# A conv + GRU kernel: which DMA queues carry the first x chunks, the biases and the weights

## The chip, the cores and the metric

The kernel runs on one core of a Trainium2 chip. The metric is the device time of one execution in microseconds (us), given as the median of several runs. Profiles are of one execution; in them, times count from the first instruction.

PE is TensorE (matmuls; PEld its weight loads), DVE is VectorE, ACT is ScalarE, POOL is GpSimd, SP is SyncE. SP and ScalarE issue DMAs on hardware queues, POOL on the software queue.

## The reference

For 16 sequences of 256 time steps and 512 channels, all in float32: a causal depthwise convolution over time with 16 taps, a residual, a GRU whose first state is `cond`, and a second residual. B = 16 batches, and the 16 rows of `cond_2048` are both the taps of the convolution and the first states.

```
x = x + conv(x, cond_2048[:, None, :])          # 16 taps, depthwise, causal
def cell(h, x):
    gi = x @ W_ih + b_ih
    gh = h @ W_hh + b_hh
    i_r, i_z, i_n = split(gi, 3); h_r, h_z, h_n = split(gh, 3)
    r = sigmoid(i_r + h_r); z = sigmoid(i_z + h_z)
    n = tanh(i_n + r * h_n)
    return (1 - z) * n + z * h
x = x + scan(cell, cond_2048, x)                # 256 steps in sequence
```

x is (16, 256, 512), W_ih and W_hh are (512, 1536), the biases are (1536,).

## The kernel before

**Tiles and stages.** Time is cut into 16 chunks of 16 steps (`CHUNKS`), 256 columns each. A chunk of x comes from memory in natural layout (`x_nat`, line 122) in 8 DMAs of 64 KB: two parities of the time step (s) by four blocks of 128 channels (j). DVE turns it into channel-major layout (`xT`, line 224, two halves of 0.7 us), ScalarE copies the last 15 steps of the chunk before in front of it (line 220) and makes the first term of the convolution (line 241), and DVE adds the other 15 taps for each of four channel blocks, 60 `tap` instructions a chunk (line 267), which gives `x1T`. For chunk 0 two of the four channel blocks are done on PE instead, with diagonal matrices that ScalarE makes from an identity (lines 290 and 294; the identity comes from POOL).

**Products.** `wih_n`, `wih_rz` and `whh[R]`, `whh[N]`, `whh[Z]` hold the weights in SBUF; each is loaded in four DMAs, one for each quarter of 32 partitions (line 173), of 256 KB, or 512 KB for `wih_rz`. Every product reads all four quarters of its weights. `ni_units` (line 322) make the n part of x1 @ W_ih for 8 steps at a time, `pair_units` (line 385) the r and z parts for two steps.

**A step** (`step`, from line 405) issues on PE, in this order: 32 products h @ W_hh for r, 32 for n, 32 for z (all line 420), then `other_products`: one or two units each of `pair_units` and `ni_units` for later steps. DVE: `seen(r)` (line 400), rn = r * h_n (446), a transpose (448), n (450), the transpose of z (459), h - n (465), and the scans that make the new h in `hist` (472). ScalarE: sigmoid of r (437), tanh (457), sigmoid of z (463), evictions. The next step's r product needs the new h.

**The order of the work around it** is written out by hand (manual schedule): each engine and each DMA queue runs its instructions in program order. Before step 0 come, for PE, 108 idle products, the convolution of chunk 0, the spread biases (line 364), the first `ni_units` and `pair_units`; for DVE, the turn of chunk 0, taps, the turn of chunk 1, taps. The taps and turns of later chunks go through a plan (`bulk`, class `Plan`, line 45): a list of units with a cost in us and the step by which they are due. `bulk.run(0, HEAD)` runs units up to a cost of HEAD before step 0, and `bulk_work` in each step runs some more, at the rate that the due times call for and up to `ROOM` = 2.05. `bulk_work` stands before the glance and rn of its step on DVE. A chunk's turn and first terms (`ahead`) stand among the taps of the chunk before, ahead of its last ten (`AHEAD`); only chunk 2's stand behind chunk 1's taps, due four steps later (lines 597 to 601). Chunk 2's x is loaded behind the sigmoid of z in step 1 (line 635).

**The queues before.** Of x chunk 0, parity 0 goes over SP and ScalarE in turn, parity 1 over POOL (line 144); of chunk 1, parity 0 over SP and parity 1 over POOL (line 157). Two bias rows follow on SP, the third bias on POOL (lines 158 to 164). W_ih's quarters 0 and 1 go over SP, 2 and 3 over POOL (line 184). W_hh's are issued in the program behind the convolution (lines 576 to 580): quarter 0 over SP, 1 over ScalarE, 2 and 3 over POOL, and R's quarter on ScalarE waits for the first quarter of W_ih n. At most eight DMAs of the hardware queues together, and eight of the software queue, are under way: the next one on the same semaphore waits for the one before it to land.

Of the kernel before, what the change touches and what calls it, by code (L numbers as in the profile page):

```python
# [32 lines left out]
GT = 8  # L33
R, Z, N = 0, 1, 2
CHUNKS = (16,) * 16
PAD = 108
HEAD = 11.0
SYNC = mybir.DependencyInfo(mybir.DependencyClass.Sync, mybir.DependencyReason.DATA)
Q_PE = (2, 3)
NI = 8  # L40
# [35 lines left out]
def conv_gru_kernel(  # L76
# [10 lines left out]
    nc = tc.nc  # L87
# [31 lines left out]
    def load_x(c, queues=((nc.sync,), (nc.sync,)), behind=None):  # L119

        n = CHUNKS[c]
        t = xin.tile([P, max(CHUNKS) // 2, P], F32, tag="x_nat", name=f"x_nat_{c}")
        for s in range(2):
            for j in range(NQ):
                made = queues[s][j % len(queues[s])].dma_start(  # L125
                    out=t[32 * j + B * s : 32 * j + B * s + B, 0 : n // 2],
                    in_=x[:, starts[c] + s : starts[c] + n : 2, j * P : (j + 1) * P],
                )
                if s == j == 0 and behind is not None:
                    tc.add_manual_dep(made.ins, behind.ins.name, SYNC, reason="later in time")  # L130
        x_nat[c] = t
# [8 lines left out]
    for j in range(NQ):  # L140
        (nc.sync, nc.scalar)[j % 2].dma_start(
            out=cond_nat[32 * j : 32 * j + B, :], in_=cond[:, j * P : (j + 1) * P]
        )
    load_x(0, ((nc.sync, nc.scalar), (nc.gpsimd,)))
    nc.scalar.activation(warm, warm, AF.Sigmoid)
    ident = const.tile([P, P], F32)
    make_identity(nc, ident)
# [6 lines left out]
    bn_nat = const.tile([P, P], F32)  # L154
    nc.vector.memset(bn_nat, 0.0)

    load_x(1, ((nc.sync,), (nc.gpsimd,)))
    nc.sync.dma_start(out=b_two[0:1, :], in_=b_hh.rearrange("(o c) -> o c", o=1))
    nc.sync.dma_start(
        out=b_two[1:2, 0 : 2 * C], in_=b_ih[0 : 2 * C].rearrange("(o c) -> o c", o=1)  # L160
    )
    nc.gpsimd.dma_start(
        out=bn_nat[0:P:L, :], in_=b_ih[2 * C : 3 * C].rearrange("(j c) -> j c", j=NQ)
    )

# [1 line left out]
    wih_rz = const.tile([P, NQ, 2 * C], F32)  # L167
    wih_n = const.tile([P, NQ, C], F32)
    whh = [const.tile([P, NQ, C], F32, name=f"whh_{g}") for g in range(3)]

    def load_weights(w_sb, w, g, queues):
        return [
            queues[j].dma_start(
                out=w_sb[L * j : L * j + L],
                in_=w[j * P : (j + 1) * P, g * C : g * C + w_sb.shape[2]].rearrange(
                    "(q l) c -> l q c", l=L
                ),
            )
            for j in (0, 2, 1, 3)
        ]  # L180


    for tile_of, g in ((wih_n, N), (wih_rz, R)):
        of_wih = load_weights(tile_of, w_ih, g, (nc.sync, nc.sync, nc.gpsimd, nc.gpsimd))
    zero_z = [const.tile([P, NQ * B * 2], F32, name=f"zero_z_{i}") for i in range(2)]
    for t in zero_z:
        nc.gpsimd.memset(t, 0.0)
# [26 lines left out]
    def turn_units(c):  # L214

        def halo():
            xT[c] = xtp.tile([P, NQ, HALO + CMAX], F32, tag="xT", name=f"xT_{c}")
            if c:
                m = CHUNKS[c - 1] * B
                nc.scalar.copy(xT[c][:, :, 0:HALO], xT[c - 1][:, :, m : m + HALO])  # L220

        def turn(a):
            o = HALO + a * PAIR
            nc.vector.transpose(  # L224
                xT[c][:, :, o : o + GT * B].rearrange("p q (a r) -> p a q r", r=L),
                x_nat[c][:, a : a + GP].rearrange("p a (q l) -> p a q l", q=NQ),
            )
            if 2 * (a + GP) == CHUNKS[c] and 4 < c + 3 < NCH:
                load_x(c + 3)

        return [(0.0, halo)] + [
            (0.7, lambda a=a: turn(a)) for a in range(0, CHUNKS[c] // 2, GP)
        ]

    def first_terms(c):

        x1T[c] = x1p.tile([P, NQ, CMAX], F32, tag="x1T", name=f"x1T_{c}")
        n = CHUNKS[c] * B

        def first(q):  # L240
            nc.scalar.activation(  # L241
                x1T[c][:, q, 0:n],
                xT[c][:, q, HALO : HALO + n],
                AF.Copy,
                scale=last1[:, q : q + 1],
            )

        for q in range(NQ):
            firsts.append((c, q, lambda q=q: first(q)))
# [9 lines left out]
    def tap_units(c):  # L259

        n = CHUNKS[c] * B

        def tap(k, q):
            while any(item[:2] == (c, q) for item in firsts):
                firsts.pop(0)[2]()
            to = slice(lag(k) if c == 0 else 0, n)
            nc.vector.scalar_tensor_tensor(  # L267
                out=x1T[c][:, q, to],
                in0=xT[c][:, q, k * B + to.start : k * B + n],
                scalar=condT[:, q, k : k + 1],  # L270
                in1=x1T[c][:, q, to],
                op0=ALU.mult,
                op1=ALU.add,
            )

        return [
            (0.135 + n / 960.0, lambda k=k, q=q: tap(k, q)) for k in range(K - 1) for q in range(NQ)
        ]
# [28 lines left out]
    def ni_units(t0, steps):  # L307

        n = steps * B
        c, o = chunk_of(t0)  # L310
        units = []
        hold = {}

        def prod(q, kc):
            if q == 0 and kc == 0:
                hold["ni"] = nip.tile([P, NQ, NI * B], F32, tag="ni", name=f"ni_{t0}")
                for i in range(steps):
                    ni[t0 + i] = hold["ni"][:, :, i * B : (i + 1) * B]
            if kc == 0:
                hold[q] = ps_ni.tile([P, NI * B], F32, tag="pni", name=f"pni_{t0}_{q}")  # L320
            for j in range(NQ):
                nc.tensor.matmul(  # L322
                    hold[q][32 * j : 32 * j + 32, 0:n],
                    lhsT=wih_n[:, kc, j * P + q * L : j * P + q * L + L],
                    rhs=x1T[c][:, kc, o : o + n],
                    start=(kc == 0),
                    stop=(kc == NQ - 1),
                    skip_group_check=True,
                )
            if kc == NQ - 1:  # L330
                evictions.append(lambda: evict(q))

        def evict(q):
            nc.scalar.activation(  # L334
                hold["ni"][:, q, 0:n], hold[q][:, 0:n], AF.Identity, bias=bnT[:, q, 0:1]
            )

        for q in range(NQ):
            for kc in range(NQ):
                units.append(lambda q=q, kc=kc: prod(q, kc))  # L340
        return units
# [33 lines left out]
    def seed_nh(p):  # L375
        nc.scalar.copy(nh[p % 2], b_rows[:, N])
# [160 lines left out]
    bulk = Plan()  # L537
# [21 lines left out]
    taps = [fn for i, (_, fn) in reversed(list(enumerate(tap_units(0)))) if i % NQ not in Q_PE]  # L559
# [13 lines left out]
    nc.scalar.copy(b_rows, spare)  # L573
    seed_rz(0)
    seed_nh(0)
    for g in (R, N, Z):

        made = load_weights(whh[g], w_hh, g, (nc.sync, nc.scalar, nc.gpsimd, nc.gpsimd))
        if g == R:
            tc.add_manual_dep(made[2].ins, of_wih[0].ins.name, SYNC, reason="behind W_ih in time")  # L580
    for fn in ni_units(*blocks[0]):
        while evictions:
            evictions.pop(0)()
# [5 lines left out]
    for c in range(1, NCH):  # L589
        due = starts[c] - NI  # L590
        taps = tap_units(c)

        ahead = []
        if c + 1 < NCH:
            ahead = turn_units(c + 1) + [(0.0, lambda c=c: first_terms(c + 1))]
        at = len(taps) - AHEAD
        for cost, fn in taps[:at] + (ahead if c > 1 else []) + taps[at:]:
            bulk.add(cost, due, fn)
        if c == 1:
            for cost, fn in ahead:  # L600
                bulk.add(cost, due + GT // 2, fn)
    bulk.run(0, HEAD)

    h = (lambda kc: condT[:, kc, 0:B], condT[:, :, 0:B])
# [69 lines left out]
```

## Time and profile before

| | us |
|---|---|
| median of 3 runs (lowest, highest) | 1043.94 (1042.65, 1044.66) |
| the profiled execution, as timed | 1043.13 |
| its span, first to last instruction | 1041.2 |
| PE busy, DVE busy, ACT busy, POOL busy | 1023.8, 926.6, 380.2, 11.4 |
| matmuls of line 420, r and z; n | 539.4; 269.6 |
| taps of line 267 on DVE, 930 | 377.3 |

Issue to landing before step 0, by the DMA view (medians): an x piece 4.9 us on POOL, 4.3 on SP and 4.1 on ACT, in the first 34 us; a W_hh quarter 14.2 on POOL, 15.4 on SP, 9.8 on ACT.

How to read it: a busy time is the union of an engine's instructions. A row of the timeline gives the start, the length, the engine (with a q for its sequencer, which issues DMAs), the line, the operation, what it writes and reads, and how many were merged; in brackets stands how long the engine idled before it and what ended that. A row of the windows gives the stretch, the busy time of PE, PEld, DVE, ACT and POOL with the number of instructions, the granted clock of TensorE as a share of full speed, the mean busy share of the 16 DMA engines, and the rate in GB/s.

### The profile page before, as it was taken

The page shows a single profiled execution, that of the slowest core. Times are in us where ns is not written, and L with a number is a line of the kernel's source. Part 1 is how long each engine was busy: PE and PEld are TensorE (multiplying, and loading weights), DVE is VectorE, ACT ScalarE, POOL GpSimd, SP SyncE. Part 2 cuts the span into 40 slices and gives each one's busy share as a digit, 9 for nine tenths or more (in the row PEclk, how much of TensorE's full clock was granted, in tenths as well). Part 3 has the DMA queues.
Part 4 walks back from the last instruction along what each step waited for, and adds up shares of the span by engine and source line. Part 5 has one row for each costly group of instructions (what it writes and reads, how often), then busy time and mean ns, then how long its engine had stood idle before and what let it go on. Part 6 is the DMA issues. An engine that isn't in the chain of part 4 may idle for free.

```text
span 1041.2 us, 71853 instructions
## 1 busy us (share of the span) xinstructions
PE 1023.8 (98%) x32952; PEld 929.9 (89%) x32952; DVE 926.6 (89%) x3606; ACT 380.2 (37%) x1520; POOL 11.4 (1%) x27
## 2 busy tenths in 40 slices
PE   7899999999999999999999999999999999999997
PEld 7789999999999999999999999999999999999986
DVE  7899999999999999999999999999999999996555
ACT  6243433434333343433334333343333334333332
POOL 4000000000000000000000000000000000000000
PEclk9999999999999999999999999999999999999999
DMA  9320100101010010100100010010000000000000
GB/s 232 93 60 8 32 14 20 30 15 27 13 34 15 15 34 6 34 14 15 35 15 25 15 33 16 14 33 7 14 15 14 14 13 5 15 15 14 14 11 17
DMA packets 40978, 27.72 MB, mean 27 GB/s; under 512 B 6686, under 2 KB 38498, under 8 KB 40676
## 3 DMA queue, kind: packets, MB, share of 16 engines
q1 hardware_dynamic: 38612, 18.52, 7.9%
q8 instruction: 257, 4.21, 1.8%
q0 software_dynamic: 1216, 3.67, 1.3%
q10 hardware_dynamic: 848, 0.95, 0.4%
q14 instruction: 45, 0.37, 0.1%
HBM read 14.73 MB, written 8.39 MB: 22 GB/s over the span
## 4 chain that ended last, share of the span: by engine, by line
PE 96%; DVE 1%; DMA 1%; ACT 0%; issue 0%; POOL 0%; SPq 0%; DVEq 0%; POOLq 0%
PE prz L420 42%; PE pnh L420 21%; PE prz L385 20%; PE pni L322 10%; PE conv L294 1%; DMA whh<-in_L_cond_W_hh_dram 1%; DMA x_nat<-in_x_dram 0%; DVE rnT L448 0%; DVE rn L446 0%; DVE zp L459 0%; DVE n L450 0%; DVE xT L224 0%; ACT zero_z L463 0%; POOL x_nat L125 0%; DVE hist L472 0%
## 5 line engine op out<-in xcount | busy, mean ns | idle before, releaser
L420 PE MATMUL prz<-whh,hist 128*32 128x128 f32 x16320 | 539.4, 273 | 2.2 <-DVE hist L472 1.3
L420 PEld LDWEIGHTS prz<-whh,hist 128*32 128x32 f32 x16320 | 449.7, 104 | 7.3 <-DVE hist L472 5.3
L267 DVE SCALAR_TENSOR_TENSOR x1T<-xT,condT,x1T 128x256 f32<-128x256 f32 (+2 forms) x930 | 377.3, 462 | 0.6 <-ACT x1T L241 0.6
L420 PE MATMUL pnh<-whh,hist 128*32 128x128 f32 x8160 | 269.6, 273 | 0.0
L385 PE MATMUL prz<-wih_rz,x1T 128*32 128x256 f32 x4096 | 268.0, 379 | 0.0
L420 PEld LDWEIGHTS pnh<-whh,hist 128*32 128x32 f32 x8160 | 226.5, 104 | 0.0
L457 ACT ACTIVATE dn<-n 128x64 f32<-128x64 f32 x256 | 67.9, 265 | 325.1 <-DVE n L450 325.1
L385 PEld LDWEIGHTS prz<-wih_rz,x1T 128*32 128x32 f32 x4096 | 128.4, 110 | 43.8
L322 PEld LDWEIGHTS pni<-x1T,wih_n 128*32 128x32 f32 x4096 | 122.4, 110 | 43.7 <-ACT ni L334 0.8
L437 ACT ACTIVATE r<-prz 128x128 f32<-128x128 f32 x256 | 70.9, 277 | 240.5 <-PE prz L420 237.7
L322 PE MATMUL pni<-x1T,wih_n 128*32 128x128 f32 x4096 | 157.9, 273 | 0.6 <-ACT ni L334 0.6
L472 DVE TENSOR_TENSOR_SCAN hist<-zero_z,dn 128x32 f32<-128x32 f32 (+1 forms) x768 | 128.5, 216 | 0.0
L446 DVE TENSOR_TENSOR rn<-r,pnh 128x128 f32<-128x128 f32 x256 | 72.3, 282 | 38.7 <-PE pnh L420 37.4
L463 ACT ACTIVATE zero_z<-zp 128x32 f32<-128x32 f32 x512 | 90.8, 226 | 6.9
L448 DVE STREAM_TRANSPOSE rnT<-rn 128x128 f32<-128x128 f32 x256 | 79.7, 311 | 8.8
L459 DVE STREAM_TRANSPOSE zp<-prz 128x128 f32<-128x128 f32 x256 | 80.8, 316 | 0.1
L334 ACT ACTIVATE ni<-pni,bnT 128x128 f32<-128x128 f32 x128 | 46.9, 367 | 75.7 <-PE pni L322 75.7
L465 DVE TENSOR_TENSOR dn<-hist,dn 128x64 f32<-128x64 f32 x255 | 58.3, 229 | 11.4
L450 DVE TENSOR_TENSOR n<-rnT,ni 128x64 f32<-128x64 f32 x256 | 57.6, 225 | 8.9
L400 DVE COPY glance<-r 1x1 f32<-1x1 f32 x256 | 34.1, 133 | 28.3 <-ACT r L437 28.2
L373 ACT COPY prz<-b_rows 128x256 f32<-128x256 f32 x128 | 48.6, 379 | 0.0
L400 DVE COPY glance<-zero_z 1x1 f32<-1x1 f32 x256 | 36.4, 142 | 7.9
(51 smaller groups left out, 214.6 us busy)
## 6 DMA issues: line engine op xcount, KB each, us to landing
out_dram<-o SPq DMA_DIRECT2D x248, 32.0 KB, 1.7
x_nat<-in_x_dram SPq DMA_DIRECT2D x118, 64.0 KB, 3.0
whh<-in_L_cond_W_hh_dram POOLq DMA_DIRECT2D x6, 256.0 KB, 14.2
wih_rz<-in_L_cond_W_ih_dram POOLq DMA_DIRECT2D x2, 512.0 KB, 10.9
wih_rz<-in_L_cond_W_ih_dram SPq DMA_DIRECT2D x2, 512.0 KB, 12.7
whh<-in_L_cond_W_hh_dram SPq DMA_DIRECT2D x3, 256.0 KB, 15.4
whh<-in_L_cond_W_hh_dram ACTq DMA_DIRECT2D x3, 256.0 KB, 9.8
x_nat<-in_x_dram POOLq DMA_DIRECT2D x8, 64.0 KB, 4.9
```

Of the source, the lines that this page charges most:

```text
L267: nc.vector.scalar_tensor_tensor(out=x1T[c][:, q, to], in0=xT[c][:, q, k * B + to.start : k * B + n], scalar=condT[:, q, k : k + 1], in1=x ...
L322: nc.tensor.matmul(hold[q][32 * j : 32 * j + 32, 0:n], lhsT=wih_n[:, kc, j * P + q * L : j * P + q * L + L], rhs=x1T[c][:, kc, o : o + n], ...
L385: nc.tensor.matmul(rz[p % 2][32 * j : 32 * j + 32], lhsT=x1T[c][:, kc, o : o + PAIR], rhs=w_rz[:, :, j * P : (j + 1) * P], start=False, st ...
L400: nc.vector.tensor_copy(glances[i][0:1], of_scalar[0:1, 0:1])
L420: product = nc.tensor.matmul(dst[32 * j : 32 * j + m], lhsT=h[0](kc), rhs=whh[g][:, kc, j * P : (j + 1) * P], start=False, stop=(kc == NQ ...
L437: of_r = nc.scalar.activation(r, pr, AF.Sigmoid)
L446: nc.vector.tensor_mul(rn, r, pnh)
L448: nc.vector.transpose(rnT, by_part(rn))
L457: nc.scalar.activation(dn_v[:, :, :, 1], n, AF.Tanh)
L459: nc.vector.transpose(zp, by_part(pz))
L463: nc.scalar.activation(z_v[:, qs, :, 1], zp[:, qs, half], AF.Sigmoid) for qs in halves
L472: nc.vector.tensor_tensor_scan(hist_g[:, lo + at : lo + end], z[:, to], dn[:, to], 0.0, op0=ALU.mult, op1=ALU.add,)
```

## The change

The first two chunks of x go over POOL's software queue, all 16 pieces. The three bias loads go over SP, ahead of the weights. All weights are now loaded in one loop before the rest of the program, in the order W_ih n, W_ih rz, W_hh R, N, Z: quarter 0 over SP, 2 and 3 over POOL, and quarter 1 over SP, except for W_hh N and Z, where it goes over POOL. ScalarE's queue carries no weights, and the wait of R's quarter for W_ih is gone. On POOL the identity now comes behind the eight pieces of chunk 0, and the two memsets of `zero_z` behind all weight issues. HEAD is 10 instead of 11, and chunk 2's turn and first terms stand among chunk 1's taps as in the other chunks.

In the program as built, 25 instead of 27 of chunk 1's taps stand before step 0 on DVE; steps 1 to 4 have five of them each instead of five, five, four and four, counting from the bulk work of step 1; step 5 has both halves of chunk 2's turn and one tap; steps 6, 7 and 8 have five, four and three taps. Before, the halves of that turn stood in steps 7 and 8.

```diff
-HEAD = 11.0
+HEAD = 10.0
...
-    load_x(0, ((nc.sync, nc.scalar), (nc.gpsimd,)))
+    load_x(0, ((nc.gpsimd,), (nc.gpsimd,)))
...
-    load_x(1, ((nc.sync,), (nc.gpsimd,)))
+    load_x(1, ((nc.gpsimd,), (nc.gpsimd,)))
     nc.sync.dma_start(out=b_two[0:1, :], in_=b_hh.rearrange("(o c) -> o c", o=1))
...
-    nc.gpsimd.dma_start(
+    nc.sync.dma_start(
         out=bn_nat[0:P:L, :], in_=b_ih[2 * C : 3 * C].rearrange("(j c) -> j c", j=NQ)
     )
...
     def load_weights(w_sb, w, g, queues):
-        return [
+        for j in (0, 2, 1, 3):
             queues[j].dma_start(
...
-    for tile_of, g in ((wih_n, N), (wih_rz, R)):
-        of_wih = load_weights(tile_of, w_ih, g, (nc.sync, nc.sync, nc.gpsimd, nc.gpsimd))
+    for tile_of, w, g in (
+        (wih_n, w_ih, N),
+        (wih_rz, w_ih, R),
+        (whh[R], w_hh, R),
+        (whh[N], w_hh, N),
+        (whh[Z], w_hh, Z),
+    ):
+        second = nc.gpsimd if tile_of is whh[N] or tile_of is whh[Z] else nc.sync
+        load_weights(tile_of, w, g, (nc.sync, second, nc.gpsimd, nc.gpsimd))
...
-    for g in (R, N, Z):
-
-        made = load_weights(whh[g], w_hh, g, (nc.sync, nc.scalar, nc.gpsimd, nc.gpsimd))
-        if g == R:
-            tc.add_manual_dep(made[2].ins, of_wih[0].ins.name, SYNC, reason="behind W_ih in time")
...
-        for cost, fn in taps[:at] + (ahead if c > 1 else []) + taps[at:]:
+        for cost, fn in taps[:at] + ahead + taps[at:]:
             bulk.add(cost, due, fn)
-        if c == 1:
-            for cost, fn in ahead:
-                bulk.add(cost, due + GT // 2, fn)
```

## The prediction

> **What bounds the kernel now.** I read the page's list of busy slices first (PE 9 tenths or more in all slices but the first four and the last, so 256 steps of 3.92 us are bound by PE and only the start is open), then the chain of waits over the first 40 us, then the timeline of each engine there, then the windows with the DMA share. The chain (start, us, what) says what sets the first step:
>
> ```profile
> 9.09 11.82 PE conv L294 x64
> ...
> 22.33 9.64 DMA whh<-in_L_cond_W_hh_dram
> 31.97 0.25 issue
> 32.22 2.00 PE prz L420 x29
> ```
>
> The reader is to see that the chain leaves PE, runs through one DMA, and comes back to PE: step 0 starts at 32.22, a quarter us after a piece of W_hh landed. The timeline says which piece: ScalarE's, issued at 22.33 behind its diagonals, evictions and bias copies; PE's rows, then DVE's, around it:
>
> ```profile
> 22.33 0.32 ACTq L173 DMA_DIRECT2D whh<-in_L_cond_W_hh_dram  x1
> ...
> 25.91 1.91 PE L385 MATMUL prz<-wih_rz,x1T 128*32 128x256 f32 x32
> 32.22 2.00 PE L420 MATMUL prz<-whh,condT 128*16 128x128 f32 x29 [4.40 <-DMA whh<-in_L_cond_W_hh_dram]
> ...
> 37.60 1.11 PE L420 MATMUL prz<-whh,hist 128*32 128x128 f32 x32
> ```
>
> ```profile
> 7.64 1.30 DVE L224 STREAM_TRANSPOSE xT<-x_nat 128x512 f32<-128x512 f32 x2 [3.33 <-DMA x_nat<-in_x_dram]
> ...
> 15.66 15.98 DVE L267 SCALAR_TENSOR_TENSOR x1T<-xT,condT,x1T 128x128 f32<-128x128 f32 x48
> 34.84 0.14 DVE L400 COPY glance<-r 1x1 f32<-1x1 f32 x1 [3.20 <-ACT r L437]
> 35.72 0.29 DVE L446 TENSOR_TENSOR rn<-r,pnh 128x128 f32<-128x128 f32 x1 [0.73 <-PE pnh L420]
> ```
>
> PE is done with its preparation at 27.82 and idles 4.40; DVE is done with its taps at 31.64 and idles 3.20. DVE is therefore only 3.2 us behind being the bound itself. The windows (us, busy of five engines, granted clock, DMA share, GB/s) show the transfers:
>
> ```profile
> 20.00:27.00 7.00, 6.44 (x167) 5.08 (x170) 7.00 (x19) 2.78 (x8) 0.00 (x0) 1.00 1.04 298
> 27.00:28.50 1.50, 0.82 (x16) 0.25 (x8) 1.50 (x5) 0.00 (x0) 0.00 (x0) 1.00 1.00 306
> 28.50:30.00 1.50, 0.00 (x0) 0.00 (x0) 1.50 (x5) 0.00 (x0) 0.00 (x0) 1.00 1.09 229
> 30.00:31.50 1.50, 0.00 (x0) 0.00 (x0) 1.50 (x5) 0.00 (x0) 0.00 (x0) 1.00 0.80 149
> 31.50:33.00 1.50, 0.78 (x13) 0.60 (x17) 0.15 (x1) 0.00 (x0) 0.00 (x0) 0.54 0.13 42
> ```
>
> The rate is near 300 GB/s while two queues have data and falls to 229 and 149 when ScalarE's queue is nearly alone; and the granted clock is 0.54 just when step 0 starts, so its R product takes 2.00 us where later steps take 0.87. Last, one later stall, at step 8:
>
> ```profile
> 66.66 0.51 ACT L241 ACTIVATE x1T<-xT,last 128x256 f32<-128x256 f32 x1 [0.90 <-DVE xT L224]
> 67.07 0.26 ACT L437 ACTIVATE r<-prz 128x128 f32<-128x128 f32 x1
> ```
>
> A forced half of chunk 2's transpose holds ScalarE's first term, which holds r, which holds PE's z product; from rn to rn this step takes 4.45 us (63.21 to 67.66).
>
> **The change, part by part.** Times are of the profiled execution, where step 1's first product starts at 37.60.
>
> *Weights leave ScalarE's queue.* Three issues (0.32 and 0.93 us, from 22.33) go. The first n eviction on ScalarE, at 23.72 behind them, then waits for PE alone, and PE's 0.56 wait for it at 24.14 goes: PE's preparation ends near 27.3 instead of 27.82. W_hh R's quarter becomes SP's ninth transfer, in flight by about 7 us; R must land by 28, and R's two pieces on the software queue, which stand ahead of all of N and Z, landed at 22.82 and 24.40 before. I cost R at nothing; its cover is some 3 us. So the old wait is gone, and the next in line are three: PE, DVE, and the last piece of W_hh Z.
>
> *PE.* Preparation ends about 27.3 plus what the convolution starts later (below, about 1.6, of which part runs while the matmuls are at half pace anyway): 28.5. A step is 3.92: step 1 could start at 32.4.
>
> *x over the software queue: DVE.* POOL's x pieces start at 1.30 and go out every 0.53 us, eight instead of four, so the last issue starts at 5.08 instead of 2.98. The four of before took 2.8, 3.5, 4.1 and 4.4 us to land, those from 4 to 6 us 5.5 to 5.9. Until SP's first weights (its queue now begins with the biases, whose memsets end at 2.9; weights from about 3.4) nothing competes, later they do. Bounds: 5.08+2.8 = 7.9 to 5.08+5.9 = 11.0; I take 3.9 to land, between the first and the fourth of the rows, 9.0. DVE started when the last landed at 7.37; it is 1.6 later. The identity on POOL, pushed behind the eight issues to about 6.2, delays the 16 diagonals (each 0.3 apart), but the convolution needs the first only and follows at its own pace, so it starts with xT, near 10.7: nothing. x's second chunk is through by about 15 and is wanted by DVE at 14.25+1.6: nothing, with one us of cover. DVE's 48 taps lose two of 0.40 each (12.8 us for 32): end 31.64+1.6-0.8 = 32.4. The glance and rn follow (0.07), and from rn to step 1 are 1.88 us (35.72 to 37.60): step 1 at 34.4. With the bounds 33.3 to 36.4.
>
> *The last weights.* Both chunks and W are 7.34 MB; the software queue now carries 4.72 of it, SP 2.62, with all of Z but a quarter at the software queue's end. Estimate from the windows: 0.28 MB by 4.5 us (one 64 KB piece in 0.53 us); 215 GB/s to 12 us (before 182 and 208, with half of x in 512-byte packets that took 0.05 us each against 0.25 for 4096 bytes on the software queue, by the trace's packet records); 268 to 15; 305 to about 28, where SP runs out; the remaining 0.7 MB alone at 200 (between 229 and 149): 31.5, landed by 32.4. Bounds: everything at 306 from 3 us on, 28.0; and every software landing as far from the next as before, with eight more x pieces at 0.53 and two more weight pieces at 1.5 each, 31.77+4.2+3.0 = 39.0. After the landing come 0.25 to the first product, 0.87 for z, and 1.30 (0.86+0.44 in step 1) of products behind it on PE: step 1 at 32.4+2.42 = 34.8.
>
> The latest of 32.4, 34.4 and 34.8 decides: 2.8 us earlier than 37.60. The half-rate clock, which made R take 2.00 instead of 0.87 us, costs between nothing and that 1.1; I take nothing, since the 0.56 and 0.6 us gaps of the row from 20 to 27 left the clock at 1.00 and R and N now run ahead of the wait for Z, so that PE's gap shrinks from 4.40 to about 2 us.
>
> *The plan.* 25 of chunk 1's taps run ahead instead of 27, and chunk 2's transposes move from steps 7 and 8 to step 5, where their data (issued behind step 1's z, landed eight us later at 49.30) is there four us before. Steps 1 to 4 then have five taps each; in steps 10 to 12 five taps gave rn distances of 4.01, 3.93, 3.93 and 3.81 after. From rn of step 0 to rn of step 9 it was 35.84; by these rows, with 4.08 and 3.98 of steps 1 and 2 as they are and steps 16 and 17 (3.96, 3.88: an output and three taps) for steps 8 and 9, it becomes 4.08+3.98+3.93+3.93+3.81+3.92+3.92+3.96+3.88 = 35.41: 0.4 won, mostly step 8. If the cover failed, each five-tap step would cost 0.1.
>
> *The sum*: 2.8+0.4 = 3.2 us off. The profiled execution took 1043.13 (span 1041.2 and 1.9 around it, unchanged): 1039.9. The median of the runs is 0.81 above it, so 1040.7.
>
> **Two rules against the rows.** The row: 306 GB/s with three queues at work, 149 to 229 with one. The Trainium skill, "DMA: Bandwidth & Descriptors", section "Issuing engines are not separate DMA queues", says that transfers run on the same 16 engines whoever starts them, and that another issuer saves issue time only. By it the last byte would come no earlier than now, about 33.0, and the gain would be 2.2+0.4 instead of 3.2; the row of the lone queue differs from it and I keep the row.
> The row: clock 0.54 after the idle stretch, R in 2.00 us. The skill's "TensorE: Matmul & The Clock Gate", section "Part 1: The HAM clock gate (the "warmup" mystery)", says that an idle window of about 3.4 us halves the clock. The trace agrees for the 4.40 us gap; by the rule a gap of two us costs nothing, and one that holds a whole window the 1.1 of R.
>
> **The rivals.** *x too late*: the software queue shares the engines with SP's weights, x0 lands at 11.0, and DVE takes the place of the wait. For: latencies of 5.5 in the same microseconds; DVE has only 3.2 us of idle time. Against: SP's and ScalarE's x pieces, which filled the engines from 3 us, are gone. Step 1 at 36.4, 1.2+0.4 won: 1042.3.
> *The bytes end when they ended*: the early stretch is used worse, Z lands at 34.0, step 1 at 36.4: 1042.3 too. For: the first three us carry one queue only. This is also the case in which the change hardly does what it says.
> *Slower: the software queue becomes the bound.* One mechanism: twice the x pieces and twelve weight pieces through one queue, each piece landing as far behind the other as before; Z lands at 39.0, PE waits, step 1 at 41.4: 3.8-0.4 = 3.4 lost, 1047.3. It eats the gain when Z lands at 35.6 and costs over 0.2% from 37.7. For: the software queue's pieces landed 1.2 to 3.5 apart. Against: SP's half of the engines comes free near 28.
>
> **How the numbers follow.** Forecast 0.61, x too late 0.16, bytes at the same end 0.10, slower 0.13. A measurement tells about 0.2%, 2.1 us, from no change. The forecast counts as faster, both middle rivals as the same: 0.61, 0.26, 0.13. The best bounds (DVE 33.3, no Z wait) give 4.3+0.4 off, 1039.2, and 0.5 for the spread of the runs, 1038.7; above, the middle rivals and the nearer part of the slower one: 1044.6.
>
> **What would show it.** No whh issue on ScalarE; step 0's first product before 29.5 at clock 1.0; x0 landed and DVE's first transpose near 9.0; the last wait before step 1's first product is PE on a whh DMA (Z) or on rn by DVE, and that product starts near 34.8; rn distance of step 8 near 3.96. Wrong if x0's transpose starts after 11.5, if Z lands after 35, or if step 5's transposes wait for x.

## The result, and the profile after

The changed kernel is slower: median 1050.48 us (1049.97 to 1051.6, 4 runs) against 1043.88 (1042.65 to 1044.66, 4 runs) for the kernel before on the same chip, a ratio of 1.0062 with a 95% interval of 1.0048 to 1.0076. The forecast was 1040.7, in 1038.7 to 1044.6. The profiled execution took 1050.13 us (span 1048.3), 7.0 more than before. Lines below the bias loads stand five further down: the products of a step are line 425 (420 before), `pair_units` 390 (385), the taps 272 (267), rn 451 (446).

The chain of waits of the kernel after, over the first 60 us (start, us, what):

```profile
7.70 10.53 DMA x_nat<-in_x_dram
18.22 0.28 issue
18.51 14.01 DMA wih_rz<-in_L_cond_W_ih_dram
32.52 0.28 issue
32.80 8.64 DMA whh<-in_L_cond_W_hh_dram
41.44 0.25 issue
41.69 1.91 PE prz L425 x32
43.59 1.45 PE prz L390 x16
45.05 0.44 PE pni L327 x16
45.48 0.87 PE prz L425 x32
```

There is no PE and no DVE in it from 7.70 to 41.69: it consists of three transfers of the software queue in a row. They are linked by the eight transfers that may be under way at once: a piece of x chunk 1, issued at 7.70, lands after 10.53 us, and only then does POOL issue a quarter of `wih_rz`; that lands 14 us later and lets the last quarter of W_hh Z go. In the chain, step 1's first product starts at 45.48 instead of 37.84 in the kernel before; in PE's timeline, whose rows start a little earlier because matmuls overlap, at 45.30 instead of 37.60. That is 7.7 us later, and the whole span is 7.1 us longer.

PE's timeline of the kernel after, around step 0, shows what it waits for:

```profile
32.61 1.93 PE L390 MATMUL prz<-wih_rz,x1T 128*32 128x256 f32 x32 [2.76 <-issue]
...
38.72 1.91 PE L425 MATMUL pnh<-whh,condT 128*16 128x128 f32 x32 [1.87 <-DMA whh<-in_L_cond_W_hh_dram]
41.69 1.91 PE L425 MATMUL prz<-whh,condT 128*16 128x128 f32 x32 [1.06 <-DMA whh<-in_L_cond_W_hh_dram]
...
45.30 0.95 PE L425 MATMUL prz<-whh,hist 128*32 128x128 f32 x28
```

W_hh N and Z each arrive too late, and both products take 1.91 us instead of the 0.87 of later steps. The windows of the same kernel over these two products show the granted clock (third from the end) at half:

```profile
38.50:41.50 3.00, 1.91 (x32) 1.17 (x32) 0.82 (x5) 0.00 (x0) 0.00 (x0) 0.50 0.54 119
41.50:43.50 2.00, 1.81 (x36) 1.68 (x40) 0.09 (x1) 0.26 (x1) 0.00 (x0) 0.50 0.00 0
```

DVE's timeline of the kernel after:

```profile
12.26 1.30 DVE L229 STREAM_TRANSPOSE xT<-x_nat 128x512 f32<-128x512 f32 x2 [7.83 <-DMA x_nat<-in_x_dram]
...
21.91 1.30 DVE L229 STREAM_TRANSPOSE xT<-x_nat 128x512 f32<-128x512 f32 x2 [2.96 <-DMA x_nat<-in_x_dram]
...
23.33 15.19 DVE L272 SCALAR_TENSOR_TENSOR x1T<-xT,condT,x1T 128x128 f32<-128x128 f32 x46
38.45 0.13 DVE L405 COPY glance<-r 1x1 f32<-1x1 f32 x1
40.69 0.29 DVE L451 TENSOR_TENSOR rn<-r,pnh 128x128 f32<-128x128 f32 x1 [2.11 <-PE pnh L425]
```

x chunk 0 is there at 12.14 (before 7.37), chunk 1 at 21.79 (before 11.11), and the taps end at 38.5 (before 31.64). So x costs twice: even with all weights in place, DVE would have let step 1 start only near 38.5 + 0.1 + 1.9 = 40.5. The windows of the kernel after (columns as before; the last two are the share of the 16 DMA engines and GB/s):

```profile
7.50:12.00 4.50, 0.00 (x0) 0.00 (x0) 0.00 (x0) 4.50 (x16) 2.30 (x5) 1.00 1.06 174
12.00:15.00 3.00, 1.29 (x3) 1.14 (x4) 2.67 (x6) 3.00 (x12) 1.09 (x2) 1.00 1.04 180
15.00:20.00 5.00, 5.00 (x31) 4.78 (x30) 3.95 (x13) 1.55 (x4) 1.72 (x4) 1.00 1.04 170
20.00:27.00 7.00, 6.26 (x74) 5.49 (x77) 5.09 (x21) 3.39 (x9) 3.23 (x6) 1.00 1.06 246
27.00:40.00 13.00, 7.50 (x198) 5.63 (x192) 11.59 (x31) 2.02 (x6) 1.46 (x4) 0.92 1.03 207
```

The same stretches of the kernel before, but for the one from 20 to 27 us (298 GB/s, shown in the prediction):

```profile
7.50:12.00 4.50, 2.91 (x8) 2.55 (x9) 4.29 (x11) 4.50 (x16) 3.00 (x8) 1.00 1.08 208
12.00:15.00 3.00, 3.00 (x15) 2.99 (x13) 3.00 (x10) 2.75 (x8) 1.54 (x4) 1.00 1.01 268
15.00:20.00 5.00, 5.00 (x39) 4.92 (x38) 5.00 (x21) 1.97 (x5) 0.50 (x1) 1.00 1.04 313
27.00:40.00 13.00, 8.60 (x232) 7.67 (x228) 8.87 (x29) 1.62 (x7) 0.00 (x0) 0.87 0.36 87
```

In the last of them all was nearly done. After the change the DMA engines count as fully busy throughout, yet from 7.5 to 20 us they move 170 to 180 GB/s where they moved 208 to 313, and about 200 for the 13 us in which the software queue works alone (by the packet records SP's weights are through at about 26 us). Two things need an explanation: why x is late, and why the busy engines move so little.

### The profile page after: what moved, and what is told of

Read it like the earlier page. It is cut to its first block, busy times and chain, and to the rows that moved or that the text cites. A ratio compares the mean times of both kernels' runs of the same rounds, so it can differ in the third digit from the quotient of the medians.

```text
span 1048.3 us, 71854 instructions
## 1 busy us (share of the span) xinstructions
PE 1024.2 (98%) x32952; PEld 928.4 (89%) x32952; DVE 926.5 (88%) x3606; ACT 380.7 (36%) x1520; POOL 16.1 (2%) x36
## 3 DMA queue, kind: packets, MB, share of 16 engines
q0 software_dynamic: 1600, 4.72, 2.2%
## 4 chain that ended last, share of the span: by engine, by line
PE 94%; DMA 3%; DVE 1%; POOL 1%; issue 0%; ACT 0%; DVEq 0%; POOLq 0%
PE prz L425 42%; PE pnh L425 21%; PE prz L390 20%; PE pni L327 10%; DMA wih_rz<-in_L_cond_W_ih_dram 1%; DMA x_nat<-in_x_dram 1%; DMA whh<-in_L_cond_W_hh_dram 1%; POOL x_nat L125 1%; DVE rnT L453 0%; DVE zp L464 0%; DVE rn L451 0%; ACT zero_z L468 0%; DVE n L455 0%; DVE hist L477 0%; DVE glance L405 0%
```

## The experiments

The runs came in four groups, each beside the kernel before on the same chip. A ratio is to that kernel before; x0 and x1 stand for the landing of the last piece of x chunk 0 and of chunk 1, in us.

### Which part of the change costs the time

Theories: A, x on the software queue next to SP's weights; B, the new split of the weights, with Z at the software queue's end. A1 is a form of A in which x pieces are slow because each reads rows that lie far apart in memory.

**x_only**: the kernel before, with only the 16 x pieces moved.

```diff
-    load_x(0, ((nc.sync, nc.scalar), (nc.gpsimd,)))
+    load_x(0, ((nc.gpsimd,), (nc.gpsimd,)))
...
-    load_x(1, ((nc.sync,), (nc.gpsimd,)))
+    load_x(1, ((nc.gpsimd,), (nc.gpsimd,)))
```

> The kernel before with one edit: all 16 x pieces over the software queue. Theory A (in the same microseconds, x on the software queue and weights on SP's: x is in flight longer, and everything with it): x chunk 0 lands at 11 to 12.5 instead of 7.4, the rate stays under 200 GB/s until about 20 us, and the time is 1047 to 1051, most of the loss. Theory B (only the uneven split of the weights counts, the software queue alone from 26 us): x lands near 9 and the time stays within 2 us of 1043.9.

Measured: 1052.17 us, ratio 1.0076 (1.0061 to 1.0091). x0 landed at 14.78, x1 at 25.02. DVE and PE in its timelines:

```profile
14.90 1.30 DVE L224 STREAM_TRANSPOSE xT<-x_nat 128x512 f32<-128x512 f32 x2 [10.79 <-DMA x_nat<-in_x_dram]
...
26.56 15.59 DVE L267 SCALAR_TENSOR_TENSOR x1T<-xT,condT,x1T 128x128 f32<-128x128 f32 x47
```

```profile
39.96 2.01 PE L420 MATMUL prz<-whh,condT 128*16 128x128 f32 x32 [5.54 <-DMA whh<-in_L_cond_W_hh_dram]
```

Both landings and the time are beyond what theory A expected. The move of x alone makes the whole loss: the ratio's interval overlaps that of the full change.

**x_as_before**: the reverse, the kernel after with those two lines put back.

> The changed kernel with x back on the three queues of before; biases, weights and plan as changed. Theory A: x chunk 0 lands at 7 to 8.5, the rate reaches 300 GB/s by 13 us, Z lands at 32 to 35, and the time is 1039 to 1043, faster than before. Theory B: the software queue still has 4.2 of its 4.7 MB, so only 0.5 MB at 200 GB/s, 2.6 us, is won: about 1047.9.

Measured: 1045.18 us, ratio 1.0013 (1.0003 to 1.0022). With x back on three queues about a fifth of the loss is left (1.3 of 6.2 thousandths), so B as the main cause is out; but there is no gain either, and the time lies between the two expectations. Its DMA view for 9 to 14 us shows why:

```profile
q0 software_dynamic: 275, 0.93, 102.7%
q1 hardware_dynamic: 19, 0.01, 1.5%
```

Columns are packets, MB and the share of 16 engines. Now SP's weights, queued behind x and the biases, are the ones that stand still: q1, SP's queue, moves 0.01 MB in 5 us while the software queue takes everything. PE then waits 3.86 us for `wih_rz` and 2.59 for W_hh R, and step 0 starts at 35.33 instead of 32.22, as its timeline says:

```profile
29.50 3.24 PE L390 MATMUL prz<-wih_rz,x1T 128*32 128x256 f32 x32 [3.86 <-DMA wih_rz<-in_L_cond_W_ih_dram]
35.33 1.26 PE L425 MATMUL prz<-whh,condT 128*16 128x128 f32 x29 [2.59 <-DMA whh<-in_L_cond_W_hh_dram]
```

**plan_only**: the kernel before with HEAD 10 and chunk 2's turn among chunk 1's taps, nothing else.

```diff
-HEAD = 11.0
+HEAD = 10.0
...
-        for cost, fn in taps[:at] + (ahead if c > 1 else []) + taps[at:]:
+        for cost, fn in taps[:at] + ahead + taps[at:]:
```

> The kernel before with HEAD 10 and chunk 2's turn among chunk 1's taps; queues as before. All theories: step 0 starts at 32.2 as before, the stall of step 8 goes (rn distance 3.96 instead of 4.45), 0.4 us won: 1043.1 to 1043.9.

Measured: 1044.24 us, ratio 1.000 (0.9991 to 1.0009). The plan does no harm: steps 2 to 9 take 0.4 us less from rn to rn, as forecast, which is below what the times can tell. Its queues are those of the kernel before, so its profile also shows how far two executions differ with nothing changed there: x0 landed at 8.08 and x1 at 12.19 (before 7.37 and 11.11), ScalarE's quarter of W_hh N at 34.42 (32.57), the rates from 7.5 us on were 178, 232 and 285 GB/s (208, 268, 313), and step 1 started at 39.59 (37.60). One profile for each kernel therefore does not tell landings apart that differ by less than about 2 us.

**close_rows**: the kernel after, x chunks 0 and 1 read from one batch's neighbouring rows.

```diff
-                    in_=x[:, starts[c] + s : starts[c] + n : 2, j * P : (j + 1) * P],
+                    in_=(
+                        x[2 * c + s, 0 : B * n // 2, j * P : (j + 1) * P].rearrange(
+                            "(b i) c -> b i c", b=B
+                        )
+                        if c < 2
+                        else x[:, starts[c] + s : starts[c] + n : 2, j * P : (j + 1) * P]
+                    ),
```

> The changed kernel, but the pieces of x chunks 0 and 1 are read from rows of one batch that lie 2 KB apart, 128 rows of 512 bytes for a piece, instead of 16 batches 512 KB apart: the same bytes, pieces, queues and 512-byte runs; chunks 0 and 1 so hold other values than the reference's. If the far rows make x slow (A1): the rate goes to 270 to 300 GB/s from about 5 us, x chunk 0 lands at 8 to 9.5, and the time falls to 1040 to 1045. If it is the queue's share beside SP's weights (A2): x lands at 11 to 12.5 again and the time is 1049 to 1051.

Measured: 1051.89 us, ratio 1.0074 (1.0058 to 1.0091), x0 at 14.08 and x1 at 23.94. Neighbouring rows are no faster: A1 falls.

### Halves of the partitions, or the queue

Theories: H, what is written into one half of the partitions (0 to 63 or 64 to 127) is held to about 200 GB/s, and SP's quarters (0, 1) and the software queue's (2, 3) fill different halves; Q, x pieces beside SP's weights are slow wherever they are written.

**even**: the kernel before with W_hh issued early, quarters 0 and 1 over SP and 2 and 3 over POOL; x, biases and plan as before. It is the base of two further runs.

```diff
-        of_wih = load_weights(tile_of, w_ih, g, (nc.sync, nc.sync, nc.gpsimd, nc.gpsimd))
+        load_weights(tile_of, w_ih, g, (nc.sync, nc.sync, nc.gpsimd, nc.gpsimd))
+    for g in (R, N, Z):
+        load_weights(whh[g], w_hh, g, (nc.sync, nc.sync, nc.gpsimd, nc.gpsimd))
...
-    for g in (R, N, Z):
-
-        made = load_weights(whh[g], w_hh, g, (nc.sync, nc.scalar, nc.gpsimd, nc.gpsimd))
-        if g == R:
-            tc.add_manual_dep(made[2].ins, of_wih[0].ins.name, SYNC, reason="behind W_ih in time")
```

> The kernel before, with one edit: quarter 1 of W_hh goes over SP instead of ScalarE and is issued with the other weights, so SP carries quarters 0 and 1 (partitions 0 to 63) and POOL 2 and 3 (64 to 127); x, biases and plan as before. Theory H (each half of the partitions takes about 200 GB/s, and 300 come only when two queues write to different halves): 280 to 310 GB/s from 12.5 us to the end, the last weights land at 31 to 33, DVE is the next bound, time 1039 to 1043. Theory Q (pieces of x behind weights on the software queue are slow whatever partitions they go to): the same here.

Measured: 1044.96 us, ratio 1.0001 (0.999 to 1.0011): no gain, where both theories expected 1039 to 1043. The software queue's Z landed at 33.34 and SP's last weights only at 35.68.

**same_half**: even with SP carrying quarters 0 and 2 of every weight, POOL 1 and 3. Each queue carries as many bytes as in even, but as long as the two queues stay in step both write the same half at the same time. The lines shown are against even.

```diff
-        load_weights(tile_of, w_ih, g, (nc.sync, nc.sync, nc.gpsimd, nc.gpsimd))
+        load_weights(tile_of, w_ih, g, (nc.sync, nc.gpsimd, nc.sync, nc.gpsimd))
...
-        load_weights(whh[g], w_hh, g, (nc.sync, nc.sync, nc.gpsimd, nc.gpsimd))
+        load_weights(whh[g], w_hh, g, (nc.sync, nc.gpsimd, nc.sync, nc.gpsimd))
```

> As even, but SP carries quarters 0 and 2 and POOL 1 and 3, in that order, so that both queues write to partitions 0 to 63 and then both to 64 to 127, as long as they stay in step; the same bytes, sizes and queues' loads. Theory H: near 200 GB/s where they are in step (up to 300 where they drift apart), the last weights land 3 to 8 us later than in even, and the time is 3 to 8 us longer. Theory Q: nothing changes, within 1 us of even.

Measured: 1048.62 us, ratio 1.003 (1.0019 to 1.0041). The windows of even:

```profile
15.00:20.00 5.00, 5.00 (x37) 4.92 (x37) 5.00 (x22) 1.98 (x5) 0.91 (x3) 1.00 1.04 274
20.00:27.00 7.00, 7.00 (x174) 5.92 (x176) 7.00 (x18) 2.83 (x8) 0.00 (x0) 1.00 1.03 285
```

and of same_half:

```profile
15.00:20.00 5.00, 5.00 (x39) 4.92 (x38) 5.00 (x21) 1.97 (x5) 0.90 (x3) 1.00 1.05 211
20.00:27.00 7.00, 5.87 (x150) 4.95 (x149) 7.00 (x19) 2.83 (x8) 0.00 (x0) 1.00 1.04 224
```

Same queues, same bytes, same busy engines (1.03 to 1.05): 274 and 285 GB/s where the halves differ, 211 and 224 where they meet. The last weights come at 40.18 instead of 35.68, and the intervals of the two times do not overlap. H holds for weights.

**x_upper** and **x_lower**: the kernel after with all pieces of x chunks 0 and 1 written to partitions 64 to 127, or to 0 to 63 where SP's weights go; the other half is filled with zeros.

```diff
-                    out=t[32 * j + B * s : 32 * j + B * s + B, 0 : n // 2],
+                    out=(
+                        t[
+                            64 + 32 * (j % 2) + B * s : 64 + 32 * (j % 2) + B * s + B,
+                            (j // 2) * (n // 2) : (j // 2 + 1) * (n // 2),
+                        ]
+                        if c < 2
+                        else t[32 * j + B * s : 32 * j + B * s + B, 0 : n // 2]
+                    ),
...
+    for c in (0, 1):
+        nc.vector.memset(x_nat[c][0:64, 0:GT], 0.0)
```

The lines shown are those of x_upper; x_lower has 0 in place of 64 and clears 64 to 128.

> The changed kernel, but the 16 pieces of x chunks 0 and 1 all land in partitions 64 to 127 (two columns' blocks beside each other) and partitions 0 to 63 are set to zero: the same pieces, queues and bytes from memory; the first two chunks hold other values. SP's weights of the same time go to partitions 0 to 63. Theory H: the pieces do not meet SP's weights: all of chunk 0 lands by 8.5 to 9.5 us, chunk 1 by 14 to 16, the rate from 7.5 to 15 is 230 or more, and the last weights land 4 or more us earlier than in the changed kernel (41.4). Theory Q: chunk 0 lands at 11 to 12.5, the last weights at 40 to 43.

> As x_upper, but all pieces land in partitions 0 to 63, with SP's weights, and 64 to 127 are set to zero. Theory H: chunk 0 lands after 13, chunk 1 after 22, the rate stays at or under 200 until SP is through, and the last weights land at 42 or later. Theory Q: the same landings as x_upper within 1 us.

Measured: 1051.5 us, ratio 1.0057 (1.0035 to 1.008), x0 at 13.89, x1 at 23.47; and 1054.6 us, ratio 1.0087 (1.0067 to 1.0107), x0 at 14.55, x1 at 25.85. Away from SP's half, x is as late as ever, later even than Q expected: H does not explain x, Q stands. In the half that meets SP's, x0 is 0.7 and x1 2.4 us later and the last weights land at 45.20 instead of 42.64. That is little more than the spread of two executions, so whether the half also matters for x is left open.

### What holds an x piece

Theories: S0, the pieces are slow on their own; S, each piece has its price beside SP's weights; B (here), its bytes have. L, against H: one queue alone can move only 200 GB/s, wherever it writes.

**hold**: the kernel after, SP's first weight made to wait until the last piece of x chunk 1 has landed.

```diff
-    load_x(1, ((nc.gpsimd,), (nc.gpsimd,)))
+    last_x = load_x(1, ((nc.gpsimd,), (nc.gpsimd,)))
...
-            queues[j].dma_start(
+            made = queues[j].dma_start(
...
+            if w_sb is wih_n and j == 0:
+                tc.add_manual_dep(made.ins, last_x.ins.name, SYNC, reason="behind x in time")
```

> The changed kernel with one wait more: SP's first weight waits until the last piece of x chunk 1 has landed; queues, sizes and bytes as changed. Theory Q (pieces of x on the software queue are slow because SP's weights are under way in the same microseconds): every x piece lands 2.8 to 4 us behind its issue, chunk 0 by 8 to 9 us, chunk 1 by 12 to 14, although SP's weights start 9 us later; the last weights land at 34 to 37 instead of 41.4, and the time is 1042 to 1046. Rival S0 (the software queue by itself lands a piece only every 1.4 us): chunk 0 lands at 11 or later again, the last weights at 42 or later, and the time is 1050 or more.

Measured: 1049.46 us, ratio 1.0038 (1.0025 to 1.0051). x0 landed at 8.81 and x1 at 13.45. The DMA view gives the median time to landing of single issues; first the kernel after, for the x pieces issued before 4 us, from 4 to 6 and from 6 to 9, each in its own answer:

```profile
x_nat<-in_x_dram POOLq DMA_DIRECT2D x5, 64.0 KB, 3.0
...
x_nat<-in_x_dram POOLq DMA_DIRECT2D x4, 64.0 KB, 6.1
...
x_nat<-in_x_dram POOLq DMA_DIRECT2D x5, 64.0 KB, 9.8
```

then hold, for the pieces issued from 4 to 10 us and SP's weights issued from 13 to 20:

```profile
x_nat<-in_x_dram POOLq DMA_DIRECT2D x12, 64.0 KB, 3.6
...
wih_n<-in_L_cond_W_ih_dram SPq DMA_DIRECT2D x2, 256.0 KB, 12.6
```

With SP silent each of the 16 pieces lands 2.8 to 3.7 us behind its issue, with up to seven under way at once; with SP's weights in flight those issued from 4 us on take 6 to 11. S0 falls, and Q is shown for the landings. Its last weights (34 to 37) and its time (1042 to 1046) did not come. The chain of hold says why:

```profile
9.81 3.64 DMA x_nat<-in_x_dram
...
16.02 23.57 DMA whh<-in_L_cond_W_hh_dram
```

In turn SP's weights, which come second here, wait for the software queue: the trace's packet records have no packet of SP's weights until 20 us, 6.5 us after the first issue. That ate much of what the early x had won; the last weights came at 39.6. So x in time is not enough: with x0 and x1 where the prediction had them, or earlier, the kernel is still slower than the kernel before.

**pieces8**: the kernel after, chunks 0 and 1 in 8 pieces of 128 KB instead of 16 of 64.

```diff
-    load_x(0, ((nc.gpsimd,), (nc.gpsimd,)))
+    both = const.tile([P, max(CHUNKS), P], F32, name="x_nat_01")
+    for s in range(2):
+        for j in range(NQ):
+            nc.gpsimd.dma_start(
+                out=both[32 * j + B * s : 32 * j + B * s + B],
+                in_=x[:, s : CHUNKS[0] + CHUNKS[1] : 2, j * P : (j + 1) * P],
+            )
```

> The changed kernel, but x chunks 0 and 1 come in 8 pieces of 128 KB (16 steps of one parity) instead of 16 of 64 KB, all on the software queue as there; chunk 0 is whole only with the eighth. Theory S (beside SP's weights a piece costs about 1.4 us whatever its size): the eighth lands at 14 to 17 instead of chunk 1's 21.8, and the last weights 4 or more us earlier than 41.4. Theory B (the queue gets a share of bytes or packets): the eighth lands at 20 to 23, the last weights at 40 to 43.

Measured: 1050.13 us, ratio 1.0052 (1.004 to 1.0065); the eighth piece landed at 17.90, between the two expectations, and the last weights at 37.96, 3.5 us earlier than in the kernel after and also between them. The run does not decide between S and B.

**wide**: the kernel after, each weight DMA writing one slot of all 128 partitions. The rows of W then lie in other partitions, so the products are not those of the reference.

```diff
-                out=w_sb[L * j : L * j + L],
-                in_=w[j * P : (j + 1) * P, g * C : g * C + w_sb.shape[2]].rearrange(
-                    "(q l) c -> l q c", l=L
-                ),
+                out=w_sb[:, j],
+                in_=w[j * P : (j + 1) * P, g * C : g * C + w_sb.shape[2]],
```

> The changed kernel, but each weight DMA writes 128 partitions (128 rows of W, 2 or 4 KB each) instead of 32 partitions with four rows each: the same bytes, packets, queues and order; the rows lie in other partitions, so products use permuted rows of W. Theory H (a queue alone is held at 200 GB/s by the half of the partitions that it writes to): the software queue alone, behind SP's end, moves 270 or more, and the last weights land at 35 to 38. Theory L (a lone queue moves 200 whatever it writes to): 195 to 215 GB/s in the tail, the last weights at 40 to 43. x beside SP's weights stays slow in both, unless the ports that SP's weights fill are what slows it: then chunk 0 lands before 11.

Measured: 1045.23 us, ratio 1.0001 (0.9989 to 1.0013). Its window, to be set beside 246 and 207 GB/s of the kernel after (in the packet records the software queue has 2.72 of the 2.75 MB of this stretch, so it works alone):

```profile
20.00:27.00 7.00, 7.00 (x140) 6.35 (x142) 7.00 (x27) 3.81 (x10) 2.58 (x7) 1.00 1.03 394
```

The last weights landed at 30.32 instead of 41.44, so a lone queue is not held to 200 GB/s; how many partitions its transfers write makes the difference. L falls. x remained late (10.90 and 19.25). By the expectation, x0 before 11 would mean that the ports filled by SP's weights slow it; 10.90 meets that by 0.1 us and is only 1.2 us earlier than in the kernel after, less than the spread of two executions, so this stays open. DVE became the bound, as the PE timeline of wide says:

```profile
37.76 1.94 PE L423 MATMUL prz<-whh,hist 128*32 128x128 f32 x32 [3.48 <-DVE hist L475]
```

That is step 1, 0.2 us from where the profile of the kernel before has it.

### A version meant to beat both

**even_wide**: x over three queues and W_hh early, as in even, with each weight DMA writing one slot of all partitions, and the rows taken in the order that the products need.

```diff
-                out=w_sb[L * j : L * j + L],
-                in_=w[j * P : (j + 1) * P, g * C : g * C + w_sb.shape[2]].rearrange(
-                    "(q l) c -> l q c", l=L
-                ),
+                out=w_sb[:, j],
+                in_=w[:, g * C : g * C + w_sb.shape[2]].rearrange(
+                    "(j q l) c -> q j l c", q=NQ, l=L
+                )[j],
```

> The kernel of even (the kernel before, W_hh issued early with quarter 1 over SP; x, biases and plan as before), with each weight DMA bringing the rows for one slot q of all 128 partitions instead of all slots of 32 partitions, in the layout that the program reads, so that it computes the reference. What the runs so far point to: x stays ahead of the weights in each queue, and no queue is held to the half of the partitions that it writes. Theory H: the rate after 15 us is over 300 GB/s and stays there to the end, the last weights land by 31 instead of 35.7; DVE (idle 3.20 us before the glance of step 0 in the kernel before) then becomes the bound, step 0's rn near 32.7-33.5 instead of 35.72, step 1 near 34.6-35.4 instead of 37.60: 1040.8-1042. Rival: weights that write all partitions meet x's writes in every port, x1 lands at 13-15 instead of 11.1 and DVE's taps end 2 us later; rn near 35 and 1043-1044, no gain that can be told.

Measured: 1075.71 us, ratio 1.0292 (1.0275 to 1.0308). Neither expectation came near. Its windows and SP's timeline:

```profile
20.00:27.00 7.00, 2.94 (x46) 1.92 (x48) 7.00 (x19) 1.43 (x4) 1.03 (x3) 0.73 1.11 115
34.00:46.00 12.00, 1.10 (x12) 0.22 (x12) 0.00 (x0) 0.00 (x0) 0.00 (x0) 0.50 0.26 101
```

```profile
10.36 43.13 SPq L173 DMA_DIRECT2D whh<-in_L_cond_W_hh_dram  x6
```

From 34 us on only a quarter of the DMA engines' time is used (0.26) at 101 GB/s, and SP needs 43 us to issue six transfers. Besides the queues of x and of some weights, the difference to wide is the source of a weight transfer: four groups of 32 rows with gaps, where wide has 128 rows in one run. The Trainium skill, "DMA: Bandwidth & Descriptors", section "Why a DMA increments its semaphore by 16 and not by 1", says that the number of engines that share a transfer is the largest number up to 16 that divides the outermost dimension of both sides; here these are 4 and 128, so 4 engines. The share of 0.26, some four of 16 engines, fits that; which engines were used is not in the records, and no run changed this alone. Whether H can be turned into a gain with rows in this order is left open.

## Why the prediction was wrong, point by point

| step of the prediction | forecast | measured |
|---|---|---|
| x0 landed | 9.0 (7.9 to 11.0) | 12.14 |
| x1 through | about 15 | 21.79 |
| rate to 12 us; to 15; to about 28 | 215; 268; 305 GB/s | 172-174; 180; 170, then 246 |
| rate of the lone queue | 200 GB/s | 207 |
| left for the lone queue | 0.7 MB, from 28 | 2.9 MB, from 26 |
| W_hh R landed | before 28 | 35.11 |
| DVE's taps end | 32.4 | 38.5 |
| W_hh Z landed | 32.4 (28.0 to 39.0) | 41.44 |
| Z landed to step 1 (chain) | 2.42 us | 4.04 |
| plan | 0.4 won | 0.38 won, steps 2 to 9 |

**The step that failed is the sizing of a landing without what is in flight beside it.** It stands in two terms of the sum.

*x*: "I take 3.9 to land, between the first and the fourth of the rows". Those rows were of pieces with x on the other queues beside them. Once SP has no x, its weights are in flight from about 5 us: by the packet records 0.74 MB of them from 5 to 11 us, where the kernel before has 0.26 MB, all behind 7.9 us. The x pieces issued from 4 us on then need 6 to 11 us (hold against after). The bound of 11.0 used the 5.9 of the slowest row, which had only those 0.26 MB beside it.

*The last weights*: "305 to about 28, where SP runs out; the remaining 0.7 MB alone at 200". SP ran out at about 26, but by then the software queue had moved only 1.8 of its 4.72 MB, and the other 2.9 MB took it 15 us alone. This term set the time: by DVE's path step 1 could have started near 40.5. The term of 34.8 also adds up pieces of the chain, where step 1 of the kernel before starts at 37.84, and subtracts from the timeline's 37.60; that is 0.2 us.

x_only shows that the move of x makes the loss, by both terms together. x in time alone does not turn the sign: in hold x0 landed at 8.81, within the forecast, and the time was still 1.0038 of the kernel before.

**The rates were taken as a matter of how many queues have work** ("near 300 GB/s while two queues have data"). same_half and wide show otherwise: two queues reach 211 to 224 GB/s when they write the same half, one queue 394 when it writes all partitions. The number for the lone queue, 200, was right, for the wrong reason: it is the rate of transfers that write one half. Theory H is what the Trainium skill says in "SBUF — State Buffer", section "Door 1: The DMA port swizzle": the bandwidth follows from how many of 16 ports the partitions reach, and 0 to 63 reach only half of them. The rows 285, 224 and 394 agree with it.

**The rule weighed there**, that a second issuer adds no bandwidth, holds against the row that was kept: a lone queue moved 394 GB/s in wide, and moving W_hh's quarter off ScalarE won no time in even (1.0001). The gain of 2.2+0.4 that it still allowed did not come either, since the queues do matter in another way, which neither the rule nor the prediction had: whose data was in flight first moved most of the bytes. From 5 to 15 us of the kernel after the packet records show 1.37 MB of SP's weights and 0.38 MB of the software queue. In x_as_before (9 to 14 us: 0.93 MB of the software queue, 0.01 of SP's) and in hold (13.5 to 20 us: 1.31 and none) it was the other way round.

**"I cost R at nothing; its cover is some 3 us."** R's last quarter came 7 us after 28: the software queue's R stood behind x and W_ih, so the landing of before (24.40), with eight x pieces ahead of it instead of 16, did not carry over.

**The half-rate clock "costs between nothing and that 1.1; I take nothing".** With N and Z each a gap, the clock was 0.50 for N and for Z: 1.04 us for Z and 0.59 for the products behind it, which is 1.6 of the 4.04 against 2.42. By the rule weighed there a gap of two us would have cost nothing; here PE's idle stretch before N was 1.87 us and that before Z 1.06, and the clock was 0.50 all the same from 38.5 to 43.5 us. The measurement decides against that reading of the rule.

**The rivals.** "x too late" named the mechanism, sharing with SP's weights, but stopped at 11.0. "The software queue becomes the bound" named the place, Z at 39.0 and step 1 at 41.4: the place was right, the price too low by 2.4 us of landing and the 1.6 of the clock. Both happened at once, and the prediction treated them as alternatives.

**The sum of what was measured**: step 1 is 7.70 us later by the timelines, rn of step 1 7.50 later, rn of step 9 7.12 later after the plan's 0.38, and the span 7.1 longer.

**Open**: why a piece of 64 KB waits so long beside another queue's backlog. pieces8 did not tell a price for each piece from one for bytes. Nor do the runs say how a queue keeps another out: in hold the records from 13.5 to 20 us show 48 to 50 packets of 4 KB a us for the software queue and none for SP, though SP had issued its first weights at 13.46.

## What to carry to other kernels

A transfer's time to landing holds only for what was in flight beside it; when a change takes small urgent pieces off a queue, ask first what that queue will now start earlier. For weights, look at which partitions each transfer writes before counting queues: transfers that run at the same time should write different halves, or all 128 partitions in one run of rows. And bounds of two rivals that share a cause have to be added, not chosen between.

## What was not expected of the hardware

DMA engines that count as fully busy moved anything from 115 GB/s (even_wide, 20 to 27 us) to 394 (wide, the same stretch): the share says that packets are in the engines, not that bytes move. A queue with a backlog can hold another one at next to nothing: 0.01 MB in 5 us in x_as_before. And even_wide, whose weight transfers read 4 x 32 rows where wide's read 128 in one run, took 30 us longer than wide (1075.71 against 1045.23); no run shows the price of that alone.
